# Bringing the LSTM result back to token order: PE transposes and adds, or VectorE block transposes, transfers and an accumulating load

## The chip, the cores and the metric

The kernel runs on one core of a Trainium2 chip. The metric is the device time in microseconds of one execution; the kernel before took 2464.67, 2465.80 and 2465.47 us in three runs, median 2465.47. The engines are named as in the profile: PE (TensorE), DVE (VectorE), ACT (ScalarE), POOL (GpSimd) and SP (SyncE, which only issues transfers).

## The reference, cut to what matters

x is (128, 64, 256) in float32: 128 batches of 64 nodes with 256 features, 8192 tokens in all. Four layers follow each other, each with a layernorm and a residual sum:

```
h = max(layernorm(x), 0);  x = x + L0(h, adj)   # two graph layers, then four LSTMs over windows of nodes
h = max(layernorm(x), 0);  x = x + L1(h, adj)   # attention with 4 heads and the mask of adj
h = max(layernorm(x), 0);  x = x + L2(h, adj)   # graph layer, two linear layers with batchnorm
h = max(layernorm(x), 0);  x = x + L3(h, adj)   # three graph layers
layernorm(x) = (x - mean) / sqrt(var + 1e-5)
```

The change touches the residual sum of the first layer, x + L0(h, adj), and the layernorm of the second.

## The kernel before, in words

Everything is float32. The 8192 tokens are cut into 16 groups of 512 (`GT` = 4 tiles of 128 tokens). In token form a group is a tile `x{g}` of [128 tokens, 4, 256 features]. The LSTM works in feature form: its state and result lie in four tiles `hs[i]` of [128 features, 2, 64 nodes, 32 batches], each of which holds four groups.

A recorder keeps the program order of each engine by its own estimate of when things are due; `issue_after` and `keep_in_program_order` hold some instructions behind others. The engines then run their lists strictly in order. SP's list is the queue of nearly all transfers. A tile with one buffer (`bufs=1`) is written again only when all its readers are done.

The stages, by the time in the profile: the two graph layers (to about 164 us), the four LSTMs with windows of 1, 2, 3 and 4 nodes (to about 1212 us), attention (to about 1445 us), then layers 2 and 3.

The groups come back from feature form to token form in `to_residual` (L250). For one group ACT and POOL each copy one half of the features from `hs` into `hc` (L255), reordering nodes and batches. PE turns `hc` in 8 transposes of 128x128 (L262) into two banks of PSUM. DVE adds each bank to the x tile (L266), which must hold the input x by then. Groups 0 to 3 are done in the last quarter of the LSTM of window 4 (its second pair of units, steps t = 1 and 2), one per step and unit; their x tiles have been resident since the first layer. Groups 4 to 15 are done in attention: the round for group g loads x of group g + 5 by one transfer of 512 KB (`load_x`, L58) and turns group g + 3.

A round of attention, for group g, is on PE: the values of the first half of the tokens (`values`, L837), queries and keys as seven products instead of eight (L815), the turned softmax of the group before (L898), the values of the second half, the transposes of L262, the transposes of the next layernorm's result (L127), the attention output of the group before (L911) and the scores (L862). Each half of the values is copied by ACT from PSUM into `vt` (L842, one buffer), and SP issues four transfers (L845) that rearrange it into `v`.

Around this DVE adds the products, masks, subtracts the maximum, and takes the layernorm's statistics of group g + 2 (L92, L94). In `ln_scale` DVE then adds eps (L95), POOL raises it to -0.5 (L96), and DVE forms the shift, -mean * rstd, in one scalar_tensor_tensor (L98); ACT applies scale and shift (L111). `add_output` adds the attention output to x: DVE divides by the softmax sum (L923), POOL adds (L926). `features` copies the turned layernorm (ACT, L278) and forms four differences for the seven products on DVE (`differences`, L206). At the end of the LSTM, SP loads the attention weights wqkv (L725) and DVE forms their sums (L731 to L733).

Of the kernel before, what the change touches and what calls it, by code (L numbers as in the profile page):

```python
# [8 lines left out]
F32 = mybir.dt.float32  # L9
# [5 lines left out]
P = 128  # L15
D = 256
# [22 lines left out]
def adj_preln_kernel(ctx: ExitStack, tc: tile.TileContext, x_in, adj, vec, bg0, bg1,  # L39
# [207 lines left out]
        for i in range(NTOK // (HB * NODES))  # L247
    ]

    def to_residual(g, x, pool, bufs):  # L250

        b0 = (g % PER) * GB
        hc = pool.tile([P, 2, GB, NODES], F32, tag="hc", name="hc", bufs=bufs)
        for c, copy in enumerate((nc.scalar.copy, nc.gpsimd.tensor_copy)):
            copy(hc[:, c], hs[g // PER][:, c, :, b0 : b0 + GB].rearrange("p n b -> p b n"))  # L255
        hf = hc.rearrange("p c b n -> p c (b n)")
        for k in range(2):
            ps = bank((P, 2, D))
            for t in range(2):
                tok = (2 * k + t) * P  # L260
                for c in range(2):
                    nc.tensor.transpose(  # L262
                        ps[:, t, c * P : (c + 1) * P], hf[:, c, tok : tok + P], ident
                    )
            xk = x[:, 2 * k : 2 * k + 2, :]
            nc.vector.tensor_tensor(xk, xk, ps, ALU.add)  # L266


    keep = ctx.enter_context(tc.tile_pool(name="keep", bufs=1))
# [3 lines left out]
    def features(pss):  # L273

        nonlocal last_copy
        hT, t = hTs[:, 0], hTs[:, 1].rearrange("p a (b n) -> p (a b) n", n=HN)
        for c in range(2):
            last_copy = nc.scalar.copy(hT[:, c, :], pss[c])  # L278
        blocks = [[hT[:, c, n * HN : (n + 1) * HN] for n in range(2)] for c in range(2)]
        ts = [t[:, i] for i in range(4)]  # L280
        differences(nc.vector, *blocks[0], *blocks[1], *ts, negate=True)
        return hT, (*blocks, ts)

    with tc.tile_pool(name="lw", bufs=5) as lw:
# [220 lines left out]
        with tc.tile_pool(name="back", bufs=1, reuse_waits="tile") as back_pool, \  # L505
# [196 lines left out]
            for p, nk in ((1, 8), (2, 8), (3, 7), (4, 8)):  # L702
                n = nk * HB
                wi, wh = w_next
                if p < 4:
                    w_next = (load_w(wih, p), load_w(whh, p))
                starts = range(0, NODES // p // nk * nk, nk)
                units = [(tiles, k0) for tiles in ((0, 1), (2, 3)) for k0 in starts]

                for j in range(0, len(units), 2):  # L710
                    two = [unit(p, *u, nk) for u in units[j : j + 2]]
                    first_steps(p, n, two, units[j : j + 2], w0)
                    if p > 1:
                        flush()
                        if j == 0:
                            ws, last_sum = blocks_of(p, wi, wh)
                    if j + 2 == len(units):
                        if p < 4:
                            w0 = first_blocks(
                                w_next[0], weight_tile(),  # L720
                                [copied_of[i] for i in (9, 14, 15, 15)] if p == 1 else None,
                            )
                        else:
                            w_att = weight_tile()
                            nc.sync.dma_start(  # L725
                                out=w_att[:, :, 0:768], in_=wqkv.rearrange("(c p) f -> p c f", p=P)
                            )
                            wqk = [[w_att[:, c, m * D : (m + 1) * D] for c in range(2)] for m in range(2)]
                            wv = w_att[:, :, 512:768]
                            ss = [w_att[:, c, 768:1024] for c in range(2)]  # L730
                            nc.vector.tensor_tensor(ss[0], wqk[1][0], wqk[1][1], ALU.add)  # L731
                            nc.vector.tensor_tensor(ss[1], ss[0], wqk[0][0], ALU.subtract)
                            nc.vector.tensor_tensor(wdiff, wqk[0][0], wqk[1][0], ALU.subtract)  # L733
                    for t in range(1, p):
                        for i, u in enumerate(two):
                            next_step(t, p, n, u, ws, last_sum if (j, t, i) == (0, 1, 0) else None)

                            if p == 4 and j == 2 and 2 * t + i - 2 < NK:
                                to_residual(2 * t + i - 2, xs[2 * t + i - 2], back_pool, 1)
                            if p == 4 and j == 2 and t == p - 1 and i == 0:  # L740

                                h = back_pool.tile([P, GT, D], F32, tag="hc", name="h")
                                ln_relu(xs[0], h)
                                hTs = keep.tile([P, 2, 2, GN], F32, tag="arena", name="hT")
                                hT = features(transposed(h))

    xpool_b = ctx.enter_context(tc.tile_pool(name="xres_b", bufs=1, reuse_waits="tile"))
    for g in range(NK, NG):
        xs.append(xpool_b.tile([P, GT, D], F32, tag=f"x{g}", name=f"x{g}"))
        if g == NK:  # L750
            load_x(xs[g], g)


    def arena(pool):
# [45 lines left out]
    with tc.tile_pool(name="att", bufs=2, reuse_waits="tile") as ap_:  # L800
        def normalized(g):
            h = ap_.tile([P, GT, D], F32, tag="h", name="h")
            ln_relu(xs[g], h)
            return h

        def queries_keys(b):
# [112 lines left out]
        def add_output(g, pss, ri):  # L919
            xv = xs[g].rearrange("p t (m q d) -> p (t m) q d", m=2, q=2)  # L920
            for par in range(2):
                o = ap_.tile([P, 2 * GT, NODES], F32, tag="o", name="o")
                last = nc.vector.tensor_tensor(  # L923
                    o, pss[par], ri[:, :, par, :].to_broadcast([P, 2 * GT, NODES]), ALU.mult
                )
                nc.gpsimd.tensor_tensor(out=xv[:, :, par, :], in0=xv[:, :, par, :], in1=o, op=ALU.add)  # L926
            return last

# [7 lines left out]
        for g in range(NG):  # L938
# [6 lines left out]
            hT_all, blocks = hT  # L945
            v = ap_.tile([P, 2 * GT, P], F32, tag="v", name="v")
            moved = values(hT_all, v, (0,))
            if g + NK + 1 < NG:
                with tc.issue_after(moved):
                    load_x(xs[g + NK + 1], g + NK + 1)  # L950
            q, k, finish = queries_keys(blocks)
            if g == 0:
                h = normalized(1)
            if last is not None:
                with tc.issue_after(finish.behind):
                    if g > 1:
                        add_output(g - 2, pss, ri)
                    sums_of()
            if last is not None:
                e, ri, v_last = last  # L960
# [3 lines left out]
            if g == NG - 1:  # L964

                w1 = w_att[:, :, 0:512]
                w2 = w_att[:, :, 512:1024].rearrange("p a (b f) -> a p b f", f=D)
                nc.sync.dma_start(out=w1, in_=w1t.rearrange("(c p) f -> p c f", p=P))
            values(hT_all, v, (1,))
            if g == 1:  # L970

                eT, turned = turn(e)
            if 0 < g <= NG - NK:
                to_residual(g + NK - 1, xs[g + NK - 1], ap_, 1)
            if g + 1 < NG:
                hT = features(transposed(h))
            if g == 0:
# [18 lines left out]
                    activated(ar_right, 1, masked_scores)  # L996
            ri_next, sub, sums_of = softmax(e_next[0])
            last = (e_next[0], ri_next, v)
            with tc.issue_after(sub):
                if g + 2 < NG:  # L1000
                    h = normalized(g + 2)
# [5 lines left out]
        with tc.issue_after(sub):  # L1007
# [1 line left out]
            mixed(1, (on_scalar, on_scalar))  # L1009
            pss_0 = hidden_products(0, w1, range(2, 4))  # L1010
            h1s.append(arena(ar_right))
            rstd, nmr, _ = ln_scale(xs[2], lambda: add_output(NG - 2, pss, ri))
        eT, turned = turn(e)
        with tc.issue_after(turned):
            ln_apply(xs[2], h1s[2][:, 0:2, :].rearrange("p a (b d) -> p (a b) d", d=D), rstd, nmr)
# [536 lines left out]
```

## Time and profile before

The span of the profiled execution, from its first to its last instruction, is 2463.8 us; its own time is not listed apart from the three runs, which lie 0.9 to 2.0 us above that span (median 1.7).

| | before |
|---|---|
| time, median of 3 runs | 2465.47 us (2464.67 to 2465.80) |
| span of the profiled execution | 2463.8 us |
| PE busy | 2445.8 us, 99% |
| DVE busy | 1549.5 us, 63% |
| ACT busy | 1142.2 us, 46% |
| POOL busy | 449.3 us, 18% |
| L262, PE transposes | 128 instructions |
| L255, copies on ACT and on POOL | 16 each, mean 1170 and 1192 ns |
| L266, adds on DVE | 32, mean 674 ns |
| L98, shift on DVE | 62, mean 431 ns |
| one round of attention, from 1242.1 to 1256.8 us | DVE busy 14.05, PE 14.23, ACT 8.70, POOL 5.90 us of 14.70 |

Matmuls are pipelined, so PE's busy share says little by itself; what a stage is bound by is read from the chain of waits, which follows the work that ended last back through what released it. A row of the chain gives the start in us, the length in us, and the engine, tile and line. "issue" is time in which the engine waited for nothing that the profile shows. The rows of one line of code give the count and the minimum, median and maximum in ns. A DMA's issue is the time that the queue's engine spends on starting it; its landing comes later.

### The profile page before, as it was taken

What the parts mean: (1) busy time and instruction counts of PE and PEld (TensorE: products, weight loads), DVE (VectorE), ACT (ScalarE), POOL (GpSimd) and SP (SyncE); (2) the same over time, 40 slices, a digit from 0 to 9 for tenths busy, and PEclk for the clock granted to TensorE, in tenths of its full rate; (3) what the DMA queues carried; (4) which work ended last, traced back from release to release, by engine and by line L of the source; (5) the groups of instructions that cost most, each with busy time, mean ns of one, the idle gap of its engine ahead of it and who ended that gap; (6) DMA issues with size and microseconds to landing.
All of it is one profiled execution on the core that took longest, in us unless ns stands there. A gap on an engine that the chain in (4) does not pass through costs nothing.

```text
span 2463.8 us, 46697 instructions
## 1 busy us (share of the span) xinstructions
PE 2445.8 (99%) x19756; PEld 2093.3 (85%) x19756; DVE 1549.5 (63%) x2784; ACT 1142.2 (46%) x2042; POOL 449.3 (18%) x377
## 2 busy tenths in 40 slices
PE   9999999999999999999999999999999999999999
PEld 6678888889999998888888864487998898898888
DVE  6668866666566565566599986475655455454544
ACT  4557754444354344344466566564333323333332
POOL 4431211111111111121134331023111111101110
PEclk9999999999999999999999999999999999999999
DMA  3200000001000000000122110010000000000000
GB/s 127 94 2 1 1 18 1 1 1 35 1 1 1 1 1 1 1 13 1 32 78 71 48 36 2 1 60 1 10 10 19 10 10 18 10 10 10 18 10 18
DMA packets 48561, 48.03 MB, mean 19 GB/s; under 512 B 3680, under 2 KB 44768, under 8 KB 48352
## 3 DMA queue, kind: packets, MB, share of 16 engines
q1 hardware_dynamic: 47360, 44.23, 5.8%
q8 instruction: 155, 2.54, 0.4%
q10 hardware_dynamic: 992, 0.82, 0.1%
q14 instruction: 54, 0.44, 0.1%
HBM read 28.26 MB, written 8.39 MB: 15 GB/s over the span
## 4 chain that ended last, share of the span: by engine, by line
PE 88%; DVE 7%; ACT 2%; issue 1%; POOL 1%; DMA 1%; SPq 0%; ACTq 0%; DVEq 0%; POOLq 0%
PE ps L538 41%; PE ps L1352 16%; PE ps L1397 8%; PE ps L782 4%; PE ps L144 4%; PE ps L1316 3%; PE ps L457 2%; PE ps L481 2%; PE ps L1134 2%; PE ps L1185 2%; PE ps L815 1%; PE ps L837 1%; ACT arena L229 1%; DVE st L92 1%; POOL arena L180 1%
## 5 line engine op out<-in xcount | busy, mean ns | idle before, releaser
L538 PE MATMUL ps<-diff,s 128*128 128x256 f32 (+1 forms) x1824 | 393.5, 371 | 0.9 <-DVE diff L658 0.9
L1352 PE MATMUL ps<-arena 128*128 128x256 f32 x1792 | 392.5, 381 | 0.0
L1352 PEld LDWEIGHTS ps<-arena 128*128 128x128 f32 x1792 | 337.9, 190 | 54.0 <-issue 9.3
L538 PEld LDWEIGHTS ps<-diff,s 128*128 128x128 f32 x1824 | 345.9, 190 | 33.8 <-issue 1.6
L552 ACT ACTIVATE gates<-gates,lbias 128x512 f32<-128x512 f32 (+5 forms) x426 | 244.2, 621 | 203.2 <-DVE gates L185 147.4
L180 POOL TENSOR_TENSOR gates<-p 128x512 f32<-128x512 f32 (+1 forms) x115 | 149.6, 1301 | 878.7 <-DVE p L177 827.8
L538 PE MATMUL ps<-h,w 128*128 128x256 f32 (+1 forms) x1028 | 241.0, 371 | 0.0
L538 PE MATMUL ps<-diff,w 128*128 128x256 f32 (+1 forms) x1040 | 238.7, 370 | 0.0
L538 PEld LDWEIGHTS ps<-diff,w 128*128 128x128 f32 x1040 | 197.4, 190 | 18.2
L538 PEld LDWEIGHTS ps<-h,w 128*128 128x128 f32 x1028 | 194.7, 190 | 19.0 <-issue 0.5
L552 ACT ACTIVATE gates<-ps,lbias 128x256 f32<-128x256 f32 (+3 forms) x213 | 91.6, 476 | 247.0 <-PE ps L538 246.8
L180 POOL TENSOR_TENSOR arena<-arena 128x256 f32<-128x256 f32 (+1 forms) x73 | 82.3, 1127 | 587.0 <-DVE arena L177 557.4
L229 ACT ACTIVATE arena<-arena 128x512 f32<-128x512 f32 (+1 forms) x160 | 88.6, 582 | 193.7 <-POOL arena L180 102.2
L185 DVE TENSOR_TENSOR gates<-p,ps 128x512 f32<-128x512 f32 (+1 forms) x115 | 76.4, 665 | 119.4 <-PE ps L538 119.3
L1397 PE MATMUL ps<-arena 128*128 128x128 f32 x1280 | 149.7, 276 | 0.0
L1397 PEld LDWEIGHTS ps<-arena 128*128 128x128 f32 x1280 | 145.5, 192 | 1.1
L96 POOL TENSOR_TENSOR rstd<-rstd,mhalf 128x4 f32<-128x4 f32 (+1 forms) x66 | 65.8, 998 | 423.0 <-DVE rstd L95 416.3
L185 DVE TENSOR_TENSOR arena<-arena,ps 128x256 f32<-128x256 f32 (+1 forms) x73 | 43.5, 596 | 156.9 <-PE ps L1352 87.0
L176 DVE TENSOR_TENSOR p<-p,ps 128x512 f32<-128x512 f32 (+1 forms) x131 | 86.8, 662 | 48.9 <-PE ps L538 47.9
L538 PE MATMUL ps<-state,w 128*128 128x256 f32 (+1 forms) x512 | 116.1, 370 | 0.9 <-ACT p L173 0.8
L189 DVE TENSOR_TENSOR gates<-p,ps 128x512 f32<-128x512 f32 (+1 forms) x115 | 76.7, 667 | 63.8 <-PE ps L538 63.1
L538 PE MATMUL ps<-state,s 128*128 128x256 f32 (+1 forms) x512 | 115.8, 369 | 0.0
(191 smaller groups left out, 4112.2 us busy)
## 6 DMA issues: line engine op xcount, KB each, us to landing
x<-in_x SPq DMA_DIRECT2D x27, 512.0 KB, 4.2
v<-vt SPq DMA_DIRECT2D x128, 64.0 KB, 2.1
out<-x SPq DMA_DIRECT2D x15, 512.0 KB, 2.9
w<-in_wih SPq DMA_DIRECT2D x4, 1024.0 KB, 6.3
w<-in_whh SPq DMA_DIRECT2D x3, 1024.0 KB, 4.9
arena<-in_l3w SPq DMA_DIRECT2D x3, 1024.0 KB, 5.0
w<-in_wqkv SPq DMA_DIRECT2D x1, 768.0 KB, 4.5
x<-in_x SPq DMA_DIRECT2D x2, 256.0 KB, 2.9
```

Source lines behind the costliest of these rows:

```text
L144: last = nc.tensor.matmul(pss[b][half * 64 : half * 64 + 64, c, t, :], lhsT=src[rows, t, col : col + 64], rhs=a2[rows, :], start=True, sto ...
L176: nc.vector.tensor_tensor(p1, p1, ps[2], ALU.add)
L180: nc.gpsimd.tensor_tensor(out=out[1][1], in0=p1, in1=p5, op=ALU.add)
L185: nc.vector.tensor_tensor(out[0][1], p1, ps[1], ALU.add)
L189: last = nc.vector.tensor_tensor(to, p, q, ALU.add)
L229: nc.scalar.activation(o, o, func)
L538: nc.tensor.matmul(ps[:, r], lhsT=wc[:, j, :], rhs=bc, start=first and r == 0 and c == 0, stop=True, skip_group_check=True,)
L552: nc.scalar.activation(o, ps, func, bias=lbias[:, col : col + 1])
L782: nc.tensor.matmul(ps, lhsT=w1[:, c, m * P : (m + 1) * P], rhs=a[:, 2 + c, :], start=(c == 0), stop=(c == 1),)
L1316: nc.tensor.matmul(ps[:, t, :], lhsT=w[:, t * P : (t + 1) * P], rhs=b, start=first and t == 0, stop=True, skip_group_check=True,)
L1352: nc.tensor.matmul(ps[:, r, :], lhsT=w[:, c, col : col + P], rhs=b[:, c, :], start=first and r == 0 and c == 0, stop=c == 1, skip_group_ch ...
L1397: nc.tensor.matmul(ps[:, t, :], lhsT=w[:, c, t * P : (t + 1) * P], rhs=b[:, c, :], start=first and t == 0 and c == 0, stop=c == 3, skip_gr ...
```

## The change

`to_residual` no longer uses PE, ACT, PSUM or the add on DVE. DVE turns the group in 32x32 blocks, straight from `hs` into a tile `turned` with one buffer (4 instructions of 128x256 per group). Then 16 transfers on SP, each of 32 partitions with 8 runs of 32 elements (128 bytes), put the blocks into their places in the x tile, writing over what it held. Last, POOL issues a load of the input x for that group which adds to the x tile instead of overwriting it. The plain loads of groups 4 to 15 (`load_x` in attention) are gone. In attention the turn of a group is recorded after the subtraction of the maximum, and the accumulating load one round later, behind the adds of `add_output`. In the LSTM the accumulating load follows the transfers directly.

In attention's layernorm (`normalized`) DVE only multiplies the mean by -1, and POOL multiplies by rstd. In `features` two of the four differences become one instruction of twice the size.

```
-    def to_residual(g, x, pool, bufs):
+    def to_residual(g, x, pool, tag):
         b0 = (g % PER) * GB
-        hc = pool.tile([P, 2, GB, NODES], F32, tag="hc", name="hc", bufs=bufs)
-        for c, copy in enumerate((nc.scalar.copy, nc.gpsimd.tensor_copy)):
-            copy(hc[:, c], hs[g // PER][:, c, :, b0 : b0 + GB].rearrange("p n b -> p b n"))
-        hf = hc.rearrange("p c b n -> p c (b n)")
-        for k in range(2):
-            ps = bank((P, 2, D))
-            for t in range(2):
-                tok = (2 * k + t) * P
-                for c in range(2):
-                    nc.tensor.transpose(
-                        ps[:, t, c * P : (c + 1) * P], hf[:, c, tok : tok + P], ident
-                    )
-            xk = x[:, 2 * k : 2 * k + 2, :]
-            nc.vector.tensor_tensor(xk, xk, ps, ALU.add)
+        turned = pool.tile([P, 4, GT, 2, 32], F32, tag=tag, name="turned", bufs=1)
+        for c in range(2):
+            for b in range(2):
+                nc.vector.transpose(
+                    turned[:, 2 * b : 2 * b + 2, :, c, :],
+                    hs[g // PER][:, c, :, b0 + b : b0 + GB : 2].rearrange(
+                        "p (h n) t -> p h t n", n=32
+                    ),
+                )
+        xv = x.rearrange("p t (c k j) -> p t c k j", c=2, j=32)
+        for q in range(4):
+            for k in range(4):
+                nc.sync.dma_start(
+                    out=xv[q * 32 : q * 32 + 32, :, :, k], in_=turned[k * 32 : k * 32 + 32, q]
+                )
+
+        def add_input():
+            nc.gpsimd.dma_start(out=x, in_=x_view[:, g * GT : (g + 1) * GT, :], accum_op=ALU.add)
+
+        return add_input
...
-        differences(nc.vector, *blocks[0], *blocks[1], *ts, negate=True)
+        flat = hT.rearrange("p c n -> p (c n)")
+        nc.vector.tensor_tensor(
+            t[:, 0:3:2], hT[:, :, HN:],
+            flat[:, 0 : 2 * HN].rearrange("p (a n) -> p a n", n=HN), ALU.subtract,
+        )
+        nc.vector.tensor_tensor(ts[1], blocks[1][1], ts[0], ALU.subtract)
+        nc.vector.tensor_tensor(ts[3], blocks[1][0], ts[1], ALU.subtract)
...
-                                to_residual(2 * t + i - 2, xs[2 * t + i - 2], back_pool, 1)
+                                to_residual(2 * t + i - 2, xs[2 * t + i - 2], keep, "arena")()
...
-            ln_relu(xs[g], h)
+            st, mv, rstd, nmr = (
+                lnp.tile([P, GT] + n, F32, tag=t, name=t)
+                for t, n in (("st", [6]), ("mv", [2]), ("rstd", []), ("nmr", []))
+            )
+            for t in range(GT):
+                nc.vector.bn_stats(st[:, t, :], xs[g][:, t, :])
+            for t in range(GT):
+                nc.vector.bn_aggr(mv[:, t, :], st[:, t, :])
+            nc.vector.tensor_scalar(rstd, mv[:, :, 1], LN_EPS, None, ALU.add)
+            nc.gpsimd.tensor_tensor(out=rstd, in0=rstd, in1=mhalf, op=ALU.pow)
+            nc.vector.tensor_scalar(nmr, mv[:, :, 0], -1.0, None, ALU.mult)
+            nc.gpsimd.tensor_tensor(out=nmr, in0=nmr, in1=rstd, op=ALU.mult)
+            ln_apply(xs[g], h, rstd, nmr)
...
-            if g + NK + 1 < NG:
-                with tc.issue_after(moved):
-                    load_x(xs[g + NK + 1], g + NK + 1)
...
+            if 0 < g <= NG - NK:
+                with tc.issue_after(output_added) if g > 1 else nullcontext():
+                    add_input()
...
-            if 0 < g <= NG - NK:
-                to_residual(g + NK - 1, xs[g + NK - 1], ap_, 1)
...
+            if g < NG - NK:
+                with tc.issue_after(sub):
+                    add_input = to_residual(g + NK, xs[g + NK], ap_, "turned")
```

In the list that the recorder makes for SP in attention, a round of the changed kernel mostly reads: 2 of the 16 transfers of one group, 4 of v, the other 14, 4 of v. In the LSTM, 9 of the first group's 16 stand ahead of the load of wqkv.

More of the change, by code (lines that the diff above doesn't have):

```diff
@@ L749, in adj_preln_kernel @@
         xs.append(xpool_b.tile([P, GT, D], F32, tag=f"x{g}", name=f"x{g}"))
-        if g == NK:
-            load_x(xs[g], g)
     def arena(pool):
@@ L925, in add_output @@
                 )
-                nc.gpsimd.tensor_tensor(out=xv[:, :, par, :], in0=xv[:, :, par, :], in1=o, op=ALU.add)
-            return last
+                added = nc.gpsimd.tensor_tensor(
+                    out=xv[:, :, par, :], in0=xv[:, :, par, :], in1=o, op=ALU.add
+                )
+            return last, added.ins
         wsum = ap_.tile([P, D], F32, tag="wsum", name="wsum", bufs=1)
@@ L956, in adj_preln_kernel @@
                     if g > 1:
-                        add_output(g - 2, pss, ri)
+                        _, output_added = add_output(g - 2, pss, ri)
                     sums_of()
@@ L1011, in adj_preln_kernel @@
             h1s.append(arena(ar_right))
-            rstd, nmr, _ = ln_scale(xs[2], lambda: add_output(NG - 2, pss, ri))
+            rstd, nmr, _ = ln_scale(xs[2], lambda: add_output(NG - 2, pss, ri)[0])
         eT, turned = turn(e)
```

## The prediction

> **What bounds the kernel now.** I read the page first (PE busy 99%, nearly whole chain on PE), then the chain of waits in the two stages that the diff touches: the end of the LSTM (1050 to 1212 us) and attention (1212 to 1440). In the LSTM the chain is pure PE, and the transposes of one group of 512 tokens (L262) stand in it as 0.87 us between stretches of 24.18:
>
> ```profile
> 1085.27 0.87 PE ps L262 x8
> 1086.15 24.18 PE ps L538 x112
> 1110.32 0.87 PE ps L262 x8
> ```
>
> In attention the chain changes hands. Half the rounds are held by VectorE (DVE), with a stop for GpSimd's pow inside:
>
> ```profile
> 1242.15 1.32 DVE st L92 x4
> 1244.48 1.03 POOL rstd L96
> 1245.58 1.10 issue
> 1246.68 1.27 DVE o L923 x2
> ```
>
> The same DVE row returns at 1256.85, 1271.55, 1286.24 and 1300.94: 14.7 us a round. Later rounds are all PE:
>
> ```profile
> 1390.98 1.09 PE ps L898 x8
> 1392.08 2.59 PE ps L815 x12
> 1394.67 1.73 PE ps L837 x8
> 1396.39 0.87 PE ps L262 x8
> 1397.27 0.87 PE ps L127 x8
> 1398.14 1.09 PE ps L911 x64
> 1399.23 0.93 PE ps L862 x64
> 1400.17 1.93 PE ps L837 x8
> 1402.09 3.45 PE ps L815 x16
> 1405.58 1.09 PE ps L898 x8
> ```
>
> That is 14.60 us of PE work, so PE and DVE limit attention nearly together. The third resource is the queue that issues transfers, SP. By the instructions of line 845 (the 8 transfers of v in a round, SBUF to SBUF) an issue takes, min/median/max in ns,
>
> ```profile
> L845 SPq DMA_DIRECT2D v<-vt x128: 590/605/2056, 1216.2 to 1441.7; - x128
> ```
>
> and by those of line 1438 (SBUF to DRAM, 512 KB) less:
>
> ```profile
> L1438 SPq DMA_DIRECT2D out<-x x15: 372/372/388, 1753.8 to 2424.7; - x15
> ```
>
> An issue of v costs no less after an idle stretch, so it is not backlog. The chain at the start of attention shows starts 0.65 apart, and that vt is a single buffer: the next copy to it (ACT L842) waits until the last transfer has landed.
>
> ```profile
> 1216.98 0.59 SPq L845
> 1217.63 0.60 SPq L845
> 1218.27 2.12 DMA v<-vt
> 1220.52 0.59 ACT vt L842
> ```
>
> SP's next v issue starts at 1221.14, so from the last issue of one v group to the first of the next at least 2.87 us pass.
>
> **The change, part by part.**
>
> *PE loses* 8 transposes a group, 16 groups: 0.87 each. Four are in the LSTM, -3.5 us. In attention the PE round goes from 14.60 to 13.73.
>
> *DVE, round of attention.* Gone: the x add (L266, 20 in 12.7 us from 1242 to 1389, 1.27 a round) and the shift's stop (L98 takes 1.22 us and idles 0.54 before it; 1.6 in all with 0.17 left for the scaling by -1). Merging two subtractions of 256 columns (0.42 each) into one of 512 (0.69) gives 0.15. New: 4 block transposes of 128x256. No row shows one; 0.42 (the 128x256 tensor_tensor) is nearest, 1.22 (a 128x1024) the upper end, 0.2 the lower. At 0.42, DVE goes from 14.7 to 14.7 - 1.27 - 1.6 - 0.15 + 1.7 = 13.4, below PE. At 1.22 it would be 16.6, about the SP round found below.
>
> *POOL* gives its 1.19 us copy for the shift's multiply (1.02, the pow of the same shape): nothing on 5.9 of 14.7. ACT loses a copy of 1.2 us: off the path.
>
> *SP* is where I expect the price. Each group now issues 16 transfers of 32 partitions x 8 runs of 128 bytes, beside 8 of v. One x load goes (0.59); the accumulating load is issued by POOL. By the built order a round on SP reads: 2 block transfers, 4 of v (second half), 14 block transfers, 4 of v (first half of the next group). No row shows such a transfer. SBUF to SBUF the nearest is v: 0.65 from start to start. DRAM rows give 0.37 + 0.04 = 0.41 as the lower end; the slowest v issue, 2.06, is the upper. I take 0.65. Then SP needs 24 x 0.65 = 15.6 us a round, above PE's 13.73, and cannot always issue: vt's second copy waits for the first half's transfers, and its own 4 transfers come next. The loop is 14 x 0.65 = 9.1 (block) + 3 x 0.65 + 2.87 (v, landing, copy, next v; the 2 block transfers hide here) + 4 x 0.65 = 16.5 us against 14.7.
>
> The 12 groups fall in 11 rounds: 192 x 0.65 = 124.8, 88 v issues x 0.65 = 57.2, 10 gaps of 2.22 - 1.30 = 0.92, together 191.2. Eleven rounds before took 161.7. Of the 29.5 more, the last v group's slack is given back: the copy after it starts 3.9 us after its landing before the change, and later in the new order, where ACT does both hT copies first; I take 5.5. **Attention: +24 us.** What hides behind SP then (PE's 0.87, the shift's 1.6) brings nothing. Rounds without block transfers already had no L262 and are PE's: 0.
>
> [...] Here the row says 0.65 against 2.1 to landing, and 24 on one queue add up. [...]
>
> *LSTM.* The order puts 9 block transfers of the first group ahead of the load of wqkv (issued at 1060.27 before). The third DVE transpose ends near 1059.6; 9 x 0.65 later, 1065.5, wqkv is issued, and with 4.5 us to landing (its row) arrives at 1070.0. DVE's sum of it (L731) runs at 1065.55 now, and all of DVE queues behind it: about 4 us late. L177 (1068.90) then ends at 1073.7; PE's product that overwrites its bank starts at 1071.30. PE loses 2.4. With 0.41 per issue wqkv lands at 1067.8 and PE loses 0.5.
> Then layernorm's statistics of that group wait for the accumulating load. POOL issues it after its gate sum, near 1075. Landing has no row: at least the plain load's 4.2; above, 10.1 (the slowest x load). Behind the statistics DVE has about 5.8 us of work, pow's wait included, until the next L177 ends, which PE needs at 1083.38 + 2.4 = 1085.8. At 4.2: 1085.0, no loss. At 10.1: 5. I take 7: 1087.8, 2.0. The other three groups have a whole step of 25 us. **LSTM: -3.5 + 2.4 + 2.0 = +0.9.**
>
> The accumulating loads of attention sit on POOL between the x adds and the next pow, about 9 us of idle; each waits for its block transfers, landed some 2 us after POOL gets there. Nothing, unless POOL's own issue takes over 7 us (no row; POOL's longest operation here is 2.8).
>
> *Sum:* 2463.8 + 24 + 0.9 = 2488.7 in the profiled span. The three runs (2464.67 to 2465.8) lie about 1.7 above that span: **2490 us.**
>
> **Rivals.**
> 1. *Cheap issue; faster.* If a block transfer issues at the DRAM rows' 0.41, the loop is 14 x 0.41 + 7.42 = 13.2, below PE's 13.73. Then attention gains 11 x (14.7 - 13.8) = 10, the LSTM 3.5 less about 1: 2465.5 - 12.5 = 2453. For: the 0.37 rows have more runs (512) than v (128), so runs alone do not cost. Against: every SBUF to SBUF issue takes 0.59 or more. Between the two, at 14 x t + 7.42 = 14.7, t = 0.52, the time is unchanged: 2463 to 2470.
> 2. *The transfers themselves.* A group has 4096 packets of 128 bytes. From 1256 to 1271 us, 1680 packets held 16 engines for 26.1% of 15 us, 37 ns each. At 37 ns the block packets take 9.5 us a round and with 3.9 for the rest stay under 16.5; above 49 ns the engines decide. At 80 ns: 20.5 + 3.9 = 24.4 a round, +107: about 2570. An issue of 1.1 us would come near that (14 x 1.1 + 7.42 = 22.8 a round). Against: packets far under the mean size should not cost twice the mean.
>    [...]
> 3. *A wait moves to DVE.* `turned` has one buffer, so the next transposes wait, in DVE's order, for all 16 transfers. It is inside the 16.5 us loop: the last block transfer lands 1.5 us after its issue, while SP issues v (2.6). It decides only if a landing takes over 2.6 - 1.3; then up to 1.5 a round, +16: 2506. It is the upper end of the forecast.
>
> **How the numbers follow.** Forecast (SP bound, issue 0.6 to 0.75, with rival 3): 0.60; with 0.60 to 0.75 per block issue and the LSTM from -3.5 to +6 its own range is 2474 to 2512. Rival 1: 0.20. Near even: 0.08. Rival 2: 0.12. The likeliest is 2490; the range of 2450 to 2515 leaves out rival 2 and thin edges. A difference of 0.2%, 5 us, is about what a measurement can tell from none: faster 0.20, same 0.08, slower 0.72.
>
> **What would show it.** Right: in attention the chain names SPq and DMA v<-vt and ACT vt; rounds near 16.5 us while block transfers run and 14.7 after; PE idle about 2 us a round; block issues at 0.59 or more; a DVE wait for wqkv near 1066. Wrong: block issues at 0.37; rounds of 13.8 with PE unbroken; or DMA's share near full (rival 2), or POOL idle-free around its loads.

## The result, and the profile after

The changed kernel takes 2543.32 us (median of four runs, 2541.72 to 2544.66) against 2465.64 (2464.67 to 2466.62): ratio 1.0315, 95% interval 1.0301 to 1.0330. The sign was forecast, the size was not: 2490, with 2515 as the upper end. The profiled execution took 2543.07 us (span 2541.3).

In the page, PE loses its unbroken row of nines in one place only, and there its granted clock falls as well:

```profile
PE   9999999999999999999988899999999999999999
PEclk9999999999999999999987889999999999999999
```

The page of before has nines in all slices of this row:

```profile
PEclk9999999999999999999999999999999999999999
```

From here on a round is the time from one maximum of the softmax (DVE, tile mx, 16 of them) to the next. Up to the first maximum the changed kernel is 3.9 us ahead (1220.7 against 1224.6), the last stretch is equal, and the 15 rounds between take 300.2 us instead of 218.8: **+81.4, all of it in attention.** The first seven rounds take 14.5 to 20.9 us; from the eighth to the fourteenth the median is 23.6, where before had 14.7.

The chain of waits in one late round, which shows what a round is made of. Its rows answer to the all-PE rounds of before:

```profile
1358.91 2.08 DVE turned L257 x4
1361.00 0.14 SPq L266
...
1361.18 1.14 SPq L266
...
1362.42 4.47 DMA v<-vt
...
1366.94 0.47 PE ps L934 x2
1367.41 1.15 PE ps L860 x2
1368.56 1.04 PE ps L934 x16
1369.60 1.15 PE ps L860 x2
1370.75 1.04 PE ps L934 x14
1371.80 6.34 PE ps L838 x16
...
1378.84 1.28 DVE o L946 x2
1380.12 1.13 DVE ri L910
...
1382.55 2.07 DVE turned L257 x4
```

(L934 was L911, L860 L837, L838 L815, L946 L923; L257 are the block transposes, L266 their transfers, L868 the transfers of v, L271 the accumulating load.) Read it as a loop: DVE transposes, two block transfers go ahead of v in SP's list, v lands 4.47 us after its issue, PE does what waits for v, DVE adds the products and transposes again, 23.6 us later. Two of these lengths are strange: a landing of v took 2.1 before, and L838 x16 took 3.45 before and 6.34 here. The windows view (PE, PEld, DVE, ACT, POOL busy, then the granted clock, DMA share, GB/s) says why the second:

```profile
1342.60:1365.80 23.20, 20.02 (x188) 15.88 (x188) 13.59 (x30) 7.92 (x14) 6.24 (x6) 0.78 0.40 66
```

PE looks busy for 20 of 23.2 us, but at a mean clock of 0.78. PE has eight gaps at L934, of 3.1 to 4.5 us. Within each, or right behind it, the granted clock falls to 0.5 and stays there for 7 to 10 us: with three more falls in the early rounds and the last, 88.7 us of half clock in 11 stretches. In before's attention there is none.

The prices of the new operations in attention, by the instructions of a line (duration in ns: min/median/max):

```profile
L257 DVE STREAM_TRANSPOSE turned<-h x48: 559/588/632, 1223.1 to 1452.7; 128x256 f32<-128x256 f32 x48
L266 SPq DMA_DIRECT2D x<-turned x171: 585/609/1937, 1244.5 to 1466.5; - x171
L271 POOL DMA_DIRECT2D x<-in_x x12: 1302/1322/1344, 1239.1 to 1475.2; - x12
L825 POOL TENSOR_TENSOR nmr<-nmr,rstd x14: 199/200/203, 1228.6 to 1485.8; 128x4 f32<-128x4 f32 x14
```

And the DMA view of after, 1250 to 1460 us (issues, KB each, median us from issue to landing):

```profile
v<-vt SPq DMA_DIRECT2D x80, 64.0 KB, 2.3
x<-in_x POOLq DMA_DIRECT2D x10, 512.0 KB, 6.5
x<-turned SPq DMA_DIRECT2D x155, 32.0 KB, 2.0
```

A block transfer's issue, the number that the forecast hung on, is what was taken: 0.61, with starts 0.65 apart. The accumulating load lands after 6.5 us. By the trace's landing times, of 80 transfers of v between 1245 and 1460 us, 42 were issued while such a load was under way: median landing 3.6 us, 31 of them over 3. The other 38: median 2.1, none over 3. The windows view of the 3.3 us in which most of one such load's packets start shows the 16 DMA engines full; the packets' time adds up to 1.14 of what they have:

```profile
1361.10:1364.40 3.30, 2.48 (x87) 1.96 (x76) 3.03 (x6) 0.63 (x2) 0.00 (x0) 1.00 1.14 157
```

### The profile page after: what moved, and what is told of

Read it like the earlier page. It is cut to its first block, busy times and chain, and to the rows that moved or that the text cites. A ratio compares the mean times of both kernels' runs of the same rounds, so it can differ in the third digit from the quotient of the medians.

```text
span 2541.3 us, 46827 instructions
## 1 busy us (share of the span) xinstructions
PE 2484.3 (98%) x19628; PEld 2112.6 (83%) x19628; DVE 1550.0 (61%) x2800; ACT 1127.3 (44%) x2026; POOL 453.1 (18%) x392
## 4 chain that ended last, share of the span: by engine, by line
PE 87%; DVE 5%; DMA 3%; ACT 2%; issue 1%; SPq 1%; POOL 1%; DVEq 0%; ACTq 0%; POOLq 0%
PE ps L551 39%; PE ps L1378 15%; PE ps L1423 8%; PE ps L793 4%; PE ps L144 4%; PE ps L1342 3%; PE ps L838 2%; DMA v<-vt 2%; PE ps L494 2%; PE ps L470 2%; PE ps L1160 2%; PE ps L1211 2%; PE ps L860 1%; PE ps L934 1%; DVE turned L257 1%
## 5 line engine op out<-in xcount | busy, mean ns | idle before, releaser
L551 PEld LDWEIGHTS ps<-diff,w 128*128 128x128 f32 x1040 | 197.3, 190 | 18.7 <-DVE p L177 0.6
L551 PEld LDWEIGHTS ps<-h,w 128*128 128x128 f32 x1028 | 195.0, 190 | 19.2 <-issue 0.5
L229 ACT ACTIVATE arena<-arena 128x512 f32<-128x512 f32 (+1 forms) x160 | 88.7, 582 | 193.3 <-POOL arena L180 101.3
L189 DVE TENSOR_TENSOR gates<-p,ps 128x512 f32<-128x512 f32 (+1 forms) x115 | 76.6, 666 | 64.8 <-PE ps L551 64.2
L793 PE MATMUL ps<-arena,w 128*128 128x512 f32 x256 | 114.3, 599 | 0.0
```

The source lines that it names most:

```text
L189: last = nc.vector.tensor_tensor(to, p, q, ALU.add)
L229: nc.scalar.activation(o, o, func)
L551: nc.tensor.matmul(ps[:, r], lhsT=wc[:, j, :], rhs=bc, start=first and r == 0 and c == 0, stop=True, skip_group_check=True,)
L793: nc.tensor.matmul(ps, lhsT=w1[:, c, m * P : (m + 1) * P], rhs=a[:, 2 + c, :], start=(c == 0), stop=(c == 1),)
```

## The experiments

Theory 1: SP's list makes v late, PE's gaps follow, and the half clock after them multiplies the loss. Rival 2: the accumulating load's traffic makes v land late, wherever it stands in SP's list. Rival 3: DVE's transposes lengthen a loop through DVE, whatever SP does. The recorder plans anew for each edit; where a run kept the lists of the other engines, instruction for instruction, it is marked "same lists". In the table, 15 rounds and late rounds (median of the 8th to 14th) are from the profiled execution, as is the half clock within attention.

| run | time, us | ratio to before (95%) | 15 rounds | late round | half clock, us |
|---|---|---|---|---|---|
| before | 2465.64 | | 218.8 | 14.7 | 0 |
| after | 2543.32 | 1.0315 (1.0301, 1.0330) | 300.2 | 23.6 | 88.7 |
| lstm_only | 2463.88 | 0.9993 (0.9984, 1.0002) | 219.1 | 14.7 | 0 |
| side_only | 2466.79 | 1.0005 (0.9996, 1.0014) | 220.3 | 15.0 | 0 |
| lstm_and_diff | 2467.66 | 1.0010 (1.0001, 1.0019) | 223.6 | 15.1 | 0 |
| no_acc (same lists) | 2511.50 | 1.0187 (1.0172, 1.0201) | 266.5 | 18.4 | 34.1 |
| plain_load (same lists) | 2528.27 | 1.0253 (1.0236, 1.0270) | 284.7 | 20.8 | 64.8 |
| filled (same lists) | 2546.99 | 1.0335 (1.0317, 1.0352) | 301.1 | 20.6 | 17.1 |
| filled_less (same lists) | 2522.45 | 1.0232 (1.0217, 1.0248) | 278.8 | 19.0 | 23.9 |
| v_first | 2546.64 | 1.0330 (1.0313, 1.0348) | 303.5 | 22.8 | 92.2 |
| halves | 2512.15 | 1.0187 (1.0172, 1.0202) | 268.9 | 19.2 | 23.9 |
| halves_busy | 2550.51 | 1.0348 (1.0331, 1.0365) | 312.8 | 21.0 | 10.2 |
| v_first_no_acc | 2515.94 | 1.0203 (1.0188, 1.0219) | 269.0 | 19.1 | 30.7 |
| v_on_act | 2506.92 | 1.0169 (1.0153, 1.0185) | 261.5 | 17.8 | 10.2 |
| no_acc_v_on_act (lists of v_on_act) | 2507.38 | 1.0166 (1.0151, 1.0182) | 260.8 | 17.2 | 0 |
| late_turn_v_on_act | 2508.41 | 1.0170 (1.0155, 1.0185) | 259.6 | 17.3 | 6.8 |
| late_turn_half_v_on_act | 2503.39 | 1.0152 (1.0137, 1.0167) | 257.3 | 17.0 | 6.8 |
| late_turn_halves | 2514.24 | 1.0197 (1.0182, 1.0212) | 270.2 | 18.7 | 37.5 |
| two_vt | 2499.73 | 1.0141 (1.0126, 1.0156) | 256.5 | 18.0 | 30.7 |
| two_vt_no_acc (lists of two_vt) | 2483.93 | 1.0077 (1.0063, 1.0091) | 242.1 | 16.9 | 17.1 |

### The parts by themselves

**lstm_only**: the kernel before, groups 0 to 3 the new way, attention the old.

```
-                                to_residual(2 * t + i - 2, xs[2 * t + i - 2], back_pool, 1)
+                                to_residual_new(2 * t + i - 2, xs[2 * t + i - 2], keep, "arena")()
```

> The kernel before, with the new way for groups 0 to 3 alone (in the LSTM); attention goes the old way. If the LSTM's part is a gain and the whole loss is in attention: 2461 to 2464 (in the profile of after the LSTM ends 4.3 us earlier, 1.2 of which was there before this part), with wqkv's sum late by some us at 1066 and PE's 8 transposes gone from four steps. If the block transfers ahead of wqkv cost what I forecast (wqkv 2.4, accumulating load 2.0, less 3.5): 2466 to 2467. If part of the 78 us comes from the LSTM's state (late x tiles at the start of attention): over 2470.

Measured 2463.88: 1.8 us less, at the edge of what can be told from none (the interval reaches 1.0002). The LSTM's part is no loss that can be measured, and the 78 us do not come from it.

**side_only**: the kernel before, with `normalized` (the shift on POOL) and `features` (merged differences) from the change, nothing else.

> The kernel before, with only the shift of attention's layernorm on POOL and the two merged differences; nothing goes through block transfers. Forecast's reading (the stop for pow inside DVE's order, 1.6 us a round, was half of what held half the rounds): rounds of attention become PE's 14.6 from 14.65, so 2462 to 2465. If DVE's stop was on the path more than that: below 2460. If POOL's later shift delays ACT's layernorm and with it the transposes: 2466 to 2475.

Measured 2466.79, no difference that can be measured; its rounds are 15.0, not 14.6. DVE's stop is gone, and the chain has found another way round, through ACT:

```profile
1308.38 0.89 PE ps L262 x8
...
1309.29 1.22 ACT hc L255
1310.51 0.97 ACT hT L278 x2
```

ACT's copy of `hc` now stands ahead of the `hT` copies that DVE's differences, the mask, the maximum and at last PE wait for. By this chain, the 1.6 us went into a wait on ACT.

**lstm_and_diff**: lstm_only with the merged differences, the shift still on DVE.

> The kernel before with the two parts of the change that are not against it: the new way for groups 0 to 3 in the LSTM, and the merged differences; layernorm's shift stays on DVE and attention goes the old way. lstm_only read 0.9993 of before. If the merged instruction saves its 0.15 us in the half of the rounds that DVE holds: 2461.5 to 2463.5, a ratio near 0.9988. If DVE has slack there: as lstm_only, 2463 to 2465.

Measured 2467.66, 0.1% slower than before, a miss: the 0.15 us saved on DVE again put `hc` ahead of `hT` in ACT's list, and rounds became 15.1. No part of the change, by itself or in these sums, is a gain that a measurement can show.

### What delays v: the accumulating load

**no_acc**: the accumulating loads of attention left out.

```
             if 0 < g <= NG - NK:
                 with tc.issue_after(output_added) if g > 1 else nullcontext():
-                    add_input()
+                    pass
```

> The changed kernel without the 12 accumulating loads of attention; it leaves out the addition of the input x for groups 4 to 15. Theory 1 (SP's list alone): rounds stay SP's 16.5 to 20 and the clock still drops in most of them; 2500 to 2540. Theory 2 (the accumulating load delays v's landings): v lands 2 us after its issue again, the gaps on PE fall below 2 us, the clock stays near 1.0, and the time comes to my forecast's 2485 to 2500. If the loads cost nothing, as I forecast: 2538 to 2546.

Measured 2511.50: 31.8 us less, with the lists of all engines but POOL unchanged. "Nothing", my price for the loads, has fallen. What is left here is in part the forecast's own picture: from one first issue of v (1366.66) to the next (1383.98) the chain is SP's list, a landing of v and vt's copy, and nothing else. (The shares are those of 1366 to 1390 us.)

```profile
by line: SPq L266 38.2%; SPq L868 28.6%; DMA v<-vt 17.1%; DVE turned L257 6.5%; issue 5.6%; ACT vt L865 2.5%; DVE k L189 2.5%; DVE ri L911 0.4%; DVEq L257 0.2%; ACTq L865 0.2%
1366.66 0.64 SPq L868
...
1368.66 2.09 DMA v<-vt
...
1370.85 0.59 ACT vt L865
...
1383.98 0.64 SPq L868
```

That is 17.3 us; the forecast's loop was 16.5. One issue of 1.20 instead of 0.61 makes most of the difference.

**plain_load**: the same loads without the addition (it leaves out the LSTM's result of groups 4 to 15; the four loads in the LSTM still add).

```
-        def add_input():
-            nc.gpsimd.dma_start(out=x, in_=x_view[:, g * GT : (g + 1) * GT, :], accum_op=ALU.add)
+        def add_input(**kw):
+            nc.gpsimd.dma_start(out=x, in_=x_view[:, g * GT : (g + 1) * GT, :], **kw)
...
```

> The changed kernel with the 12 accumulating loads of attention as plain loads of the same 512 KB from the same queue at the same place; they overwrite x, so the LSTM's result of groups 4 to 15 is left out. If the harm is the traffic of 512 KB just where v and the blocks land, or the software queue: the same as the changed kernel, 2530 to 2546. If it is the accumulation itself (slower writes that also read): v lands 2 us after its issue, and the time is that without the loads, 2506 to 2520.

Measured 2528.27, between the two. Such a load lands after 5.0 us instead of 6.5, and its packets leave the DMA engines room:

```profile
1359.30:1361.40 2.10, 2.10 (x97) 2.03 (x98) 1.73 (x4) 1.13 (x3) 0.00 (x0) 1.00 0.74 239
```

So of the loads' 31.8 us, 15 belong to the addition and 17 to a plain load of 512 KB from POOL's queue just then; no run separates its bytes from its queue.

### What the half clock costs

**halves** pins two orders: the output matmuls of the second half behind the next group's first values on PE, and the blocks behind v on SP. **halves_busy** adds matmuls there to keep PE's clock up (`keep_busy`, in that run alone).

```
-                pss = attend(eT, v_last)
+                pss = attend(eT, v_last, range(2) if g < NG - 1 else range(GT))
...
+                keep_busy(pss[0], product)
+                with tc.issue_after(product):
+                    attend(eT, v_half, range(2, GT), pss)
...
-                with tc.issue_after(sub):
+                with tc.issue_after(sub), tc.issue_after(moved):
                     add_input = to_residual(g + NK, xs[g + NK], ap_, "turned")
```

> The changed kernel with two orders pinned, as the control of the next run: the second half of attention's output matmuls stands on PE behind the next group's first values, and the 16 block transfers of a group stand behind both v sets of its round. No work is added or left out. The clock's half speed after PE's gaps should still be there. Theory 1 (SP's list, multiplied by the clock): v of the first half of the next group stands behind 16 block transfers instead of 14, v of the second half no longer behind 2 of them; rounds 20 to 24, 2520 to 2550. Theory 3 (DVE's turned loop): nothing changes, 2540 to 2546.

> The control plus 12 matmuls of 128x256 a round on PE (0.216 us each by the row of the values, 2.6 us), between the next group's first values and the second half of the output matmuls; their results are overwritten. SP's list is the same as the control's. If the half clock is a cause (some 89 us of half clock in after, so up to 44 us lost where PE is on the path): the clock stays at 1.0 and, though PE has 2.6 us more to do, the time falls by 20 to 40 against the control. If it is only a mark of the gaps (PE has slack behind SP and DVE): the time is the control's within 5, or up to 28 more (11 rounds of 2.6).

Measured 2512.15 and 2550.51. The control is 31 us faster than after, a miss, and has only 24 us of half clock left, so the pair says little of the clock in after. It says that keeping PE busy without need costs: a 128x256 matmul in float32 stands in the trace as two passes of 0.216, so 12 of them are 5.2 us a round and not 2.6.

**filled** repairs the other fault of that pair: it adds matmuls to the finished lists of after and moves nothing. **filled_less**, shown here, adds half as many (6 instead of 12), in groups 5 to 13 instead of 3 to 13.

```
+    block = nc.main_func.blocks[1].instructions
+    first = [
+        i for i in block
+        if i.opcode == "Matmult" and i.debug.bass_funcname.endswith("values")
+        and i.start_tensor_calc and i.ins[1].offset == 0
+    ]
+    for i in first[5:14]:
+        at = next(k for k, j in enumerate(block) if j.name == i.name)
+        for _ in range(6):
+            block.insert(at, mybir.InstMatmult(name=nc.get_next_instruction_name(), ins=i.ins, outs=i.outs,
...
```

> The changed kernel with every engine's list as it was, but for one thing: in groups 3 to 13 the first matmul of the first half's values (128x256) is issued 13 times instead of once, into the same place, just where PE otherwise idles over 3 us for v. 12 x 0.216 = 2.6 us more for PE a round at full clock. If the half clock is a cause (89 us of half clock in after; PE's stretch between v and the next q/k sums stands in the chain with about 10 us a round at half speed, 5 at full): the clock stays at 1.0 and the time falls to 2495 to 2520. If it is only a mark of the gaps: 2538 to 2572.

> As filled, with 6 extra matmuls in groups 5 to 13 only. In the trace of filled one such matmul took 0.433 us (two passes of 0.216), so 12 were 5.2 us, twice what was said there, and its late rounds were all PE: 20.6 = 15.4 + 5.2, yet shorter than after's 23.6. Now 2.6 us a round. If the half clock is a cause: late rounds of 18 to 19.5 and 2500 to 2518. If the gaps cost by themselves, whatever the clock: 2538 to 2560.

filled measured 2546.99, within the range named for a mere mark, but with twice the work that this range assumed: 5.2 us more a round. In its late rounds PE had no gap over 0.3 us; at 20.6 us they were still 3 us shorter than after's. The early rounds lost that again. filled_less measured 2522.45, 20.9 us less than after and 4.5 above the range for a cause, late rounds 19.0. A round in its chain, to be held against the one of after above:

```profile
1359.68 2.07 DVE turned L257 x4
...
1363.21 4.68 DMA v<-vt
...
1367.94 0.33 PE ps L934 x2
1368.26 0.63 PE ps L860 x2
1368.89 0.60 PE ps L934 x16
1369.50 0.63 PE ps L860 x2
1370.13 0.60 PE ps L934 x14
1370.73 3.67 PE ps L838 x16
...
1375.09 1.28 DVE o L946 x2
```

The same loop, the same late landing (4.68), and PE's part from L934 through L838 is 6.5 us instead of 11.2. The difference, 4.7, is the difference of the late rounds, 4.6. So the half clock is a cause, not only a mark, of about 4.6 us in each late round of after.

### Orders, queues and buffers

**v_first** has the pin on SP alone, without the order on PE.

```
-                with tc.issue_after(sub):
+                with tc.issue_after(sub), tc.issue_after(moved):
                     add_input = to_residual(g + NK, xs[g + NK], ap_, "turned")
```

> The changed kernel with one pin on SP: all 16 block transfers of a group behind the second v set of its round (2 of them stood ahead of it). PE keeps after's interleaving of the output matmuls with the values. If the 2 block transfers ahead of v (they wait for DVE's transposes, so v, PE's products and the next transposes close a loop through all engines) are what stretches the late rounds from 18 to 23.6: 2505 to 2518, as with both pins. If it was PE's order: 2535 to 2548.

Measured 2546.64, no better than after: my reading that the 2 blocks ahead of v close the loop has fallen. With v ahead, the loop closes through ACT instead: the second copy to vt stands behind both `hT` copies, which wait for PE.

```profile
1388.73 0.48 ACT hT L285
...
1389.69 0.61 ACT vt L865
...
1390.32 4.68 DMA v<-vt
...
1395.05 0.47 PE ps L934 x2
```

halves and v_first have the same list on SP and differ by 34 us, by PE's list (and small things on DVE and ACT that follow from it): what counts is that on PE the values (L860), whose copy feeds the next v, stand behind output matmuls (L934) that wait for the last v. halves takes them apart.

**v_first_no_acc** adds to this the edit of no_acc.

> The pin on SP, and no accumulating loads in attention (the addition of the input x for groups 4 to 15 is left out). SP's list alone remains of what I charged: 24 issues of 0.65 and 0.9 of waiting a round. If my forecast's loop was right and only what lay on top of it was missed: 16.5 to 17 a round, 2485 to 2497. If a loop through DVE's transposes and ACT's copies bounds it above SP's own time: 17.5 to 18.5, 2503 to 2515.

Measured 2515.94, as no_acc: SP's order does not matter without the loads either.

**v_on_act** issues v from ACT; **no_acc_v_on_act** leaves out the loads as well.

```
-                        last = nc.sync.dma_start(
+                        last = nc.scalar.dma_start(
                             out=v[par * 64 : par * 64 + 64, 4 * k + b : 4 * k + 4 : 2, :],
```

> The changed kernel, with the 8 transfers of v in a round issued by ACT instead of SP. Theory 1 (v stands behind 14 block transfers in SP's list, so attention's output waits and PE idles over 3 us, which halves its clock for the next 7 to 10 us): v leaves right after ACT's copy, SP keeps 10.4 us a round, the granted clock stays at 1.0, and ACT's extra 5.2 us fits in; 2455 to 2480. Theory 2 (the accumulating load's traffic makes v land 4 to 6 us after its issue): v leaves earlier, yet still lands late in each round; 2490 to 2525. Theory 3 (DVE's transposes and their wait for turned set the round): rounds stay above 18; 2515 to 2550.

> Both edits together: no accumulating loads in attention (the addition of the input x for groups 4 to 15 is left out) and v issued by ACT. Rounds were 17 to 20 with either alone. If SP's list and the accumulating load are the whole loss: PE's 13.8 to 14.7 a round, 2452 to 2468. If ACT's issues (5.2 us a round and more where two queues issue at once) are a bound of their own: rounds stay at 16 to 17.5, 2480 to 2505.

Measured 2506.92 and 2507.38. Rounds of 17 to 18, at full clock but for 10.2 us in v_on_act, and the loads no longer matter. So the loads do not hold these rounds, and SP's issues are little of their chain (4.9% in v_on_act from 1340 to 1380 us). Without the loads and without any half clock, 42 us above before are left, more than either range said. ACT's four issues stand between its two `hT` copies, and in this round of no_acc_v_on_act the chain goes around through DVE, POOL, ACT and a landing of v, in 17.1 us (L819 are the statistics, L823 is the pow, L111 layernorm, L285 the `hT` copies):

```profile
1370.43 2.12 DVE turned L257 x4
1372.55 1.29 DVE st L819 x4
...
1374.91 1.01 POOL rstd L823
...
1376.74 1.57 ACT h L111 x3
...
1378.78 0.54 ACT hT L285
...
1379.45 2.19 DMA v<-vt
1381.64 0.58 ACT hT L285
...
1387.48 2.13 DVE turned L257 x4
```

**late_turn_v_on_act**, **late_turn_half_v_on_act** (only v's second half on ACT) and **late_turn_halves** move DVE's transposes behind the statistics.

```
-            if g < NG - NK:
-                with tc.issue_after(sub):
-                    add_input = to_residual(g + NK, xs[g + NK], ap_, "turned")
             with tc.issue_after(sub):
                 if g + 2 < NG:
-                    h = normalized(g + 2)
+                    h, shifted = normalized(g + 2)
...
+            if g < NG - NK:
+                with tc.issue_after(shifted):
+                    add_input = to_residual(g + NK, xs[g + NK], ap_, "turned")
```

> The run with v issued by ACT, and DVE's transposes moved behind layernorm's statistics of the same round (they stood ahead of them). In that run the chain closes a loop each 17.4 us: mask, maximum, transposes 2.1, statistics, pow on POOL, layernorm, transposes of it, its copies on ACT, differences on DVE, mask. If DVE's transposes lengthen that loop: 15.3 to 16 a round, 2480 to 2490. If ACT's 8 issues in a row (5.2 us and the waits for their lanes) set the round: 2500 to 2510, unchanged.

> Late transposes, and only v of the second half issued by ACT: SP then issues 16 + 4 a round, 13 us, in the order 16 blocks, 4 v; ACT 2.6 us. Nothing is left out. If SP's list, the half clock and the transposes' place are the whole loss: rounds of 14.5 to 15.5, 2463 to 2480. If the accumulating load's collision with v and blocks still costs by itself: 2485 to 2510.

> The control with the two pinned orders, and late transposes; all 24 issues stay on SP, nothing is left out. If what remained there (18.4 a round) is SP's 15.6 us plus its waits, as I forecast: 16.5 to 18, 2485 to 2510, little changed by the transposes' place. If the transposes ahead of the statistics set it: below 2480.

Measured 2508.41, 2503.39 and 2514.24. Against their counterparts (v_on_act 2506.92 for the first, halves 2512.15 for the third; the second has none) the transposes' place is worth nothing, and rival 3 has fallen for these versions. In after itself the transposes stand in the chain with 2.1 us a round, and no run moved them there. Of theory 1 the clock is left, and of rival 2 a good part; that v stands behind blocks in SP's list has lost its support with v_first.

**two_vt** gives vt a second buffer. **two_vt_no_acc** leaves out the loads as well.

```
-                vt = ap_.tile([P, 2, D], F32, tag="vt", name="vt", bufs=1)
+                vt = ap_.tile([P, 2, D], F32, tag="vt", name="vt", bufs=2)
...
-            mx = ap_.tile([P, NH, 1], F32, tag="mx", name="mx")
+            mx = ap_.tile([P, NH, 1], F32, tag="mx", name="mx", bufs=1)
```

> The changed kernel with two buffers for vt (and one for the maximum, to make room). The second copy to vt no longer waits until the first half's transfers have landed, and with it ACT's copies of the turned layernorm, which stand behind it. SP's order comes out as 8 of v, 16 blocks. If vt's one buffer is in the loop that holds rounds at 17.5 to 18.5 in every variant: 15.7 to 16.7 a round (SP's 24 issues back to back), 2475 to 2492. If it is not: 2503 to 2518, as with v first.

> Two buffers for vt, and no accumulating loads in attention (the addition of the input x for groups 4 to 15 is left out); every engine's list but POOL's is that of two_vt. In two_vt's chain a landing of v takes 5.6 us where an accumulating load runs, 2.1 elsewhere. If that collision is what is left above SP's own time: 15.7 to 17 a round, 2475 to 2490. If the loads no longer matter once v has slack: 2495 to 2503, unchanged.

Measured 2499.73 and 2483.93. two_vt is the fastest of the full versions with the new attention, 43.6 us under after, and between the two ranges that I named. Its recorded lists differ too (PE does both halves of the output matmuls together, SP issues 8 of v and then 16 blocks), so the 43.6 are not the buffer's alone. What still costs there is the collision, taken away in the pair with equal lists: 15.8 us. In two_vt's chain it is one line, with the PE gap behind it:

```profile
1383.65 0.60 SPq L868
...
1384.30 5.61 DMA v<-vt
...
1389.96 0.79 PE ps L934 x29
```

No full version with the new attention comes near before. 

## Why the prediction was wrong, step by step

*PE's 8 transposes.* Right for what they are: L262 has left the chain. That they bring nothing in attention, as forecast, no run shows by itself.

*DVE.* A block transpose takes 0.59, four 2.08, where 1.7 was taken from the 0.42 of a subtraction. The shift on POOL costs 0.20, not the 1.02 of the pow. Both small; neither decides.

*SP.* The issue was right (0.61, starts 0.65 apart, so rival 1's 0.41 is out). About one issue in ten takes 0.9 to 1.9 instead, which the forecast left out. Where SP is the bound, in no_acc, a loop of it took 17.3 us, forecast 16.5. But the forecast took that loop for the round. In the late round of after shown above the chain is on SP for 1.3 us of 23.6.

*"The accumulating loads of attention: nothing."* **This is the step that failed.** I looked at the queue that issues them (POOL's issue is 1.3 us, far under the 7 I named) and not at what else is landing then. In the late rounds the load and DVE's transposes both follow the attention output of the group before: DVE divides it and goes on to the transposes, POOL adds it to x and issues the load. So they start together, and v is issued into the load. (The last group's blocks, for which both could wait too, had landed over 3 us earlier; waits for them stand in the early rounds alone.) In the round above the load was issued at 1359.05 and landed at 1366.22; the two blocks issued at 1360.50 and 1361.18 landed at 1366.46 and 1366.68, and v's four transfers from 1366.89 on, one after the other. In before, too, 19 of 94 landings of v took over 3 us, up to 3.9, and PE had no gap over 0.52 us in its attention: there they fell into slack. The price is 31.8 us in after (no_acc), 15.8 with two vt buffers. In the 15 rounds it is 33.7 of the 57.4 us by which the forecast for attention fell short; the other 23.7 are still there in no_acc, with 34.1 us of half clock among them, and are not divided further.

*PE's idle time.* I forecast "PE idle about 2 us a round" and gave it no further price. The gaps at L934 are 3.1 to 4.5 us, and the clock falls to 0.5 with them. This term stood nowhere in the sum; filled_less, which fills most of them, takes 20.9 us off and leaves 23.9 us of half clock. It is not independent of the loads: without them the longest gap at L934 is 2.0 us and the half clock goes from 88.7 to 34.1 us. The last section has which gaps in after had a fall and which had none. The page of before showed a clock of 9 in all slices, and I did not ask what a gap would do to it.

*The order that the recorder makes.* I read SP's list from the built order, and not PE's, where the values stand behind the output matmuls that wait for v. halves against v_first: 34 us.

*Sum.* Attention was forecast at +24 and is +81.4. With the loads out and vt doubled, the 15 rounds take 242.1 us, +23.3: the forecast's number, but not by its reason, since SP's issues are only a fifth of that chain (1240 to 1450 us).

*LSTM.* Forecast +0.9; lstm_only is 1.8 us faster. The issue of wqkv was not late: DVE's third transpose ended at 1053.3 and not at 1059.6, so the 9 blocks went out before wqkv's place, at 1059.46. The load landed after 6.45, taken 7, and DVE's statistics waited for it without harm:

```profile
1059.46 5.26 DMA w<-in_wqkv
...
1070.44 6.45 DMA x<-in_x
```

In the window 1060 to 1090 PE is busy 29.79 us of 30, where 4.4 were to be lost. The trace is 3.9 us ahead after the LSTM; 1.2 of it was there at 800 us, before the changed part.

*Rival 3*, a wait for `turned` on DVE, is 5.5 us in all, three times. *Rival 2*: it charged the block transfers' own packets, and those do not fill the engines: DMA's share is 0.30 from 1371 to 1376 us, where SP issues blocks one after the other, and 0.41 over a round. But the mean hides the 3.3 us of each accumulating load, with 1.14 in the row shown. Transfers are late by that collision, not by their number.

*Still open.* What holds rounds at 17 to 18 in v_on_act and the late_turn runs. The rows show chains around all engines, a different one in each run, since the recorder plans each anew; no single edit shortened them, and I have not separated DVE's share from ACT's.

## What to carry to other kernels

Where a transfer is made late, ask what the waiting engine is ahead of: here PE gaps of 3.1 to 4.5 us cost twice, once themselves and once as the 6.8 to 10.2 us of half clock that began with them. A load that costs its queue little (here an issue of 1.3 us) can still be dear by what lands behind it (31.8 us, no_acc), so look for the small transfers that a long one will meet, above all where both follow the same step. Read the built order of every engine that the late data passes through, not only of the queue that the change loads.

## What the runs showed of the hardware that was not expected

Of the 42 transfers of v (64 KB, from SP) that were issued while a 512 KB accumulating load from POOL's queue was under way, 40 landed 0.2 to 2.6 us after that load did. They took 3.6 us at the median and up to 6.1, against 2.1 without one. They mostly wait: while the first 90% of a load's 528 packets start, SP's queue starts at most 60 packets in eight of the ten loads between 1245 and 1460 us, and 206 and 279 in the other two. The addition itself lengthens the load from 5.0 (plain_load) to 6.5 us (after).

The granted clock fell with gaps of PE, but not only where PE was idle up to the fall. All 11 stretches at 0.5 in after's attention are multiples of 3.41 us (3.41, 6.83 or 10.24). Nine of them began in a gap of 3.1 to 4.5 us or up to 0.5 us behind it. One began in a gap of 2.7 us and one 0.8 us behind a gap of 1.9, while the three gaps of 1.0 to 1.3 us had none. Of the 3.41 us before the fall at 1390.84, PE was at work for the last 0.5; of those before the fall at 1411.32, for the first 1.1. In the late rounds the clock came back after 6.8 or 10.2 us, with PE busy throughout the last 6.8.

Of 240 issues on SP between 1245 and 1460 us, 25 took 0.9 to 1.9 us where 0.6 is the rule; with v on ACT the same is seen there, up to 1.8.
